# The weighted sum of values in a sliding-window attention tile, done in two halves of places

## The chip, the cores and the metric

The kernel runs on one core of one Trainium2 chip. Its time is the device time of one execution in microseconds (us), given as the median of several executions. TensorE (PE in the profile, its weight loads PEld) multiplies matrices out of SBUF into PSUM; VectorE (DVE) and ScalarE (ACT) work element by element; GpSimd (POOL) and SyncE (SP) do little here but fill tiles and issue transfers (DMAs). PSUM has eight banks per partition; a bank holds 512 float32 numbers per partition.

## The reference, cut to what matters

One decoder layer on x of 2 batches x 512 tokens x 1024: attention, a quantised product with a context, a feed-forward block, each followed by a layer norm. The change lies in the attention alone:

```python
q = (x @ wq.T).reshape(B, N, 32, 128).transpose(0, 2, 1, 3)
k = (x @ wk.T).reshape(B, N, 8, 128).transpose(0, 2, 1, 3)
v = (x @ wv.T).reshape(B, N, 8, 128).transpose(0, 2, 1, 3)
# four query heads share a key/value head; a query i sees the keys j with j <= i and i - j < 128
s = jnp.where((j <= i) & (i - j < 128), (q @ k.T) / sqrt(128), -inf)
o = softmax(s) @ v
x = layernorm(x + o.reshape(B, N, 32 * 128) @ wo.T)
```

## The kernel before, in words

All large products are done by Strassen's scheme (`strassen`, the matmuls on line 132, named `prod`) in float32; the second attention product, with the output weights, is `y` on line 563. In the trace every float32 matmul leaves two records, each with its own weight load ahead of it: a matmul of 512 columns is two records of 512 columns. So 48 matmuls show as x96.

Attention goes over 16 groups (2 batches x 8 key/value heads); a group has four tiles of 128 query tokens (`i` = 0 to 3), and four query heads are handled at once, so a tile of probabilities is 128 x 512. For tile `i`, `scores` (lines 323 to 369) makes the scores in two pairs. Each pair takes the only buffer of the PSUM pool `ps_s`, is copied out by ACT (L348, L350) and, where the diagonal runs through, by DVE under a mask (L352); then maximum, exponential, sum and division follow (L358 to L368).

The window is 128 wide, so query place t of a tile sees t+1 keys of its own tile and 127-t keys of the tile before. The probabilities are therefore kept in a tile with exactly 128 columns: column j holds the key j of the own tile for j <= t, and the key j of the tile before for j > t.

`weigh` (lines 384 to 404) does the weighted sum one tile later. `transpose_p` turns the probabilities with four transposes into the only buffer of the PSUM pool `ps_t` (tile `pt`, L374). DVE writes `cur`, in which only the entries of keys of the own tile are left (L380, a product with the mask `keep_cur`), and ACT writes `both`, all entries (L381). Then two matmuls add up in one bank of `ps_t` (tile `o`): values of the tile before times `both` (L397), and the difference `vd` of own and earlier values times `cur` (L398), which corrects the entries that belong to the own tile. For `i` = 0 there is one matmul (L395). One ACT copy (L401) takes the result, 128 x 512, into the tile `factors`. After every second tile, `keep` forms sums for the later product on DVE (L408 to L413) and stores them through SP's queue (L424). There are 16 x 3 = 48 weighings with two matmuls and 16 with one.

Once per group, `transpose_v` (lines 305 to 312) turns the values of the next group with four transposes into the same single buffer of `ps_t` (tile `vtr`, L308); ACT copies them out whole (L310, 128 x 512), and DVE forms `vd` from the copy (L312, 128 x 384). It falls between the `pt` and the `o` of the weighing with `i` = 0, in all groups but the first set-up: `pt`, `vtr` and `o` take the one buffer in turn.

Around this, `other` (line 446) feeds in steps of the next group's projections and of the output product, so that TensorE has work while ACT and DVE do the softmax. Each engine works through its own queue strictly in the order that the framework laid down when the program was built; that order follows the framework's own estimate of when operands are ready, so it isn't the order of the Python code: in the trace, products stand between the `pt` and the `o` of a weighing.

PSUM is full: two banks `ps_p`, four `ps_y`, one `ps_s`, one `ps_t`.

Of the kernel before, what the change touches and what calls it, by code (L numbers as in the profile page):

```python
# [9 lines left out]
F32 = mybir.dt.float32  # L10
# [4 lines left out]
ALU = mybir.AluOpType  # L15
# [3 lines left out]
P = 128  # L19
# [6 lines left out]
TPB = N // P  # L26
NQ = 32
NKV = 8
G = NQ // NKV
# [11 lines left out]
RND = 8388608.0  # L41
QMID = 128.0
MASKED = -3.0e38
HQ = HALF // 2


# [134 lines left out]
class Background:  # L181
# [6 lines left out]
    def add(self, steps, share=1):  # L188

        self.queue.append([steps, share, 0])  # L190
# [18 lines left out]
def attention(nc, tc, consts, xbuf, tpool, wpool, ps_p, ps_y, dram, kept, complete, between):  # L209
# [7 lines left out]
    with ExitStack() as ctx:  # L217
        qpool = ctx.enter_context(tc.tile_pool(name="a_q", bufs=2))
        kvpool = ctx.enter_context(tc.tile_pool(name="a_kv", bufs=2))
        work = ctx.enter_context(tc.tile_pool(name="a_work", bufs=2))  # L220
        ps_s = ctx.enter_context(tc.tile_pool(name="ps_s", bufs=1, space=PSUM))
        ps_t = ctx.enter_context(tc.tile_pool(name="ps_t", bufs=1, space=PSUM))

        factors = ctx.enter_context(tc.tile_pool(name="a_factors", bufs=1)).tile([P, 7, 7, P], F32, tag="factors", name="factors")
# [36 lines left out]
        x0 = load_x(0)  # L261
        load_weight(1)

        qT, kT, vT, v, vd = {}, {}, {}, {}, {}

        def project_first(outs):

# [37 lines left out]
        def transpose_v(b, g):  # L305
            ps = ps_t.tile([P, TPB, P], F32, tag="t", name=f"vtr_{b}_{g}")
            for i in range(TPB):
                nc.tensor.transpose(ps[:, i, :], vT[b, g][:, ts(i, P)], ident)  # L308
            v[b, g] = kvpool.tile([P, TPB, P], F32, tag="v", name=f"v_{b}_{g}")
            nc.scalar.copy(v[b, g], ps)  # L310
            vd[b, g] = kvpool.tile([P, TPB - 1, P], F32, tag="vd", name=f"vd_{b}_{g}")
            nc.vector.tensor_tensor(vd[b, g], v[b, g][:, 1:], v[b, g][:, : TPB - 1], ALU.subtract)  # L312

        def pieces(m):

            b, g = groups[m]
            for j in range(PAIRS):
                yield from project(m * PAIRS + j)
                if j == 0:
                    transpose_v(b, g)  # L320
                    yield

        def scores(b, g, i, meanwhile):
# [6 lines left out]
            if i == 0:  # L330
                nc.gpsimd.memset(s, MASKED)
            for pair in range(G // 2):
# [38 lines left out]
        def transpose_p(b, g, i, s):  # L371
            ps = ps_t.tile([P, G, P], F32, tag="t", name=f"pt_{b}_{g}_{i}")
            for c in range(G):
                nc.tensor.transpose(ps[:, :, ts(c, BLOCK)], s[:, c, :], ident)  # L374
            cur = work.tile([P, G, P], F32, tag="cur", name=f"cur_{b}_{g}_{i}", bufs=1)
            if i == 0:
                nc.scalar.copy(cur, ps)
                return cur, None
            both = work.tile([P, G, P], F32, tag="both", name=f"both_{b}_{g}_{i}", bufs=1)
            nc.vector.tensor_tensor(cur, ps, keep_cur.unsqueeze(1).to_broadcast([P, G, P]), ALU.mult)  # L380
            nc.scalar.copy(both, ps)  # L381
            return cur, both

        def weigh(pending, meanwhile):


            if pending is None:
                meanwhile()
                return
            b, g, i, s = pending  # L390
            cur, both = transpose_p(b, g, i, s)
            meanwhile()
            ps = ps_t.tile([P, G, P], F32, tag="t", name=f"o_{b}_{g}_{i}")
            if i == 0:
                nc.tensor.matmul(ps, v[b, g][:, 0, :], cur, start=True, stop=True)  # L395
            else:
                nc.tensor.matmul(ps, v[b, g][:, i - 1, :], both, start=True, stop=False)  # L397
                nc.tensor.matmul(ps, vd[b, g][:, i - 1, :], cur, start=False, stop=True)  # L398
            half, place = divmod(i, 2)
            keeping.drain()  # L400
            nc.scalar.copy(factors[:, 2 * half : 2 * half + 2, 2 * place : 2 * place + 2],  # L401
                           ps.rearrange("p (k j) t -> p k j t", k=2))
            if place:
                keeping.add(keep(b, g, half))

# [9 lines left out]
        def keep(b, g, half):  # L415


            own = slice(2 * half, 2 * half + 2)
            yield from left_sums(*(factors[:, own, k] for k in range(7)))
            if half:  # L420
                yield
                yield from left_sums(*(factors[:, k] for k in range(7)), True)
            for k in (3, 4, 5, 2, 6) if half else (0, 1):
                nc.sync.dma_start(out=kept[b][:, g, k], in_=factors[:, k])  # L424
            if half:
                complete.add((b, g, "kept"))
            yield

        keeping = Background()
# [4 lines left out]
        for m, (b, g) in enumerate(groups):  # L434
            if m + 2 == NKV:
                x1 = load_x(1)
            if m + 1 == NKV:

                right[1], late = strassen_right_steps(nc, tpool, x1, "t_1")
                late = list(late)  # L440
                for _ in range(2):
                    late.pop(0)()
            rest = pieces(m + 1) if m + 1 < len(groups) else iter(())
            for i in range(TPB):

                def other():
                    lump = next(rest, None)
                    if late:
                        late.pop(0)()
                        lump = LUMP  # L450
                    between(b, g, i, lump, keeping)

                s = scores(b, g, i, other)
                weigh(pending, other)
                pending = b, g, i, s
                for _ in range(STEPS - 2):
                    other()
            for _ in rest:
                pass
        weigh(pending, lambda: between(B - 1, NKV - 1, TPB, None, keeping))  # L460
        keeping.drain()


def project_out(nc, tc, b, xres, spaces, psum, kept, complete, wo_d, sums, x_d, begun):
# [20 lines left out]
    def load_right(n):  # L485
        if n < len(steps):
            k, g = steps[n]
            rights[n] = stream.tile([P, 2, 2, HQ], F32, tag="right", name=f"or_{b}_{n}")
            src = wo_d[(0, 2, 3)[k - 1]] if k <= 3 else sums[:, k - 4]
            nc.sync.dma_start(out=rights[n].rearrange("p j e c -> p j (e c)"), in_=src[:, g])  # L490

    def right_sums(n):
# [6 lines left out]
        b11, b12, b21, b22 = (right[:, j, e] for j in range(2) for e in range(2))  # L499
        t = stream.tile([P, 3, HQ], F32, tag="sums", name=f"ot_{b}_{n}", bufs=2)  # L500
        t1, t2, t4 = (t[:, j] for j in range(3))
# [17 lines left out]
    yield  # L519
    banks = [psum.tile([P, 2, HQ], F32, tag="p", name=f"y{k}_{b}") for k in range(4)]  # L520

# [3 lines left out]
    def read(k):  # L525
        w = stream.tile([P, 4, HQ], F32, tag="right", name=f"yw_{b}_{k}")
        p1, u4, u2, u3 = (w[:, j] for j in range(4))
        q1, q6, q7, q5 = banks[0][:, 0], banks[0][:, 1], banks[1][:, 0], banks[3][:, 1]
        add = lambda out, in0, in1: nc.vector.tensor_tensor(out, in0, in1, ALU.add)
        nc.scalar.copy(p1, q1)  # L530
        tc.keep_in_program_order(add(u2, q6, p1))
        add(u3, q7, u2)
        add(u4, q5, u2)
        rows = w[:, 0:2], u3.unsqueeze(1).to_broadcast([P, 2, HQ])
        grown = banks[2], banks[3]
        whole = w[:, 0:2], w[:, 2:4]
        for q in range(2):
            add(whole[q], grown[q], rows[q])
        yield LUMP
        for n, (h, e) in enumerate(grow[k][1]):  # L540
            for q in range(2):
                block = x[:, 2 * h + q, ts(e, HALF)].rearrange("p (e c) -> p e c", e=2)
                last = add(block, whole[q], block)
                if q == 0:
                    tc.keep_in_program_order(last)
            if n == 0:
                yield LUMP
# [445 lines left out]
def decoder_layer(ctx, tc, x, xT, ctx_kv, wq, wk, wv, wo, s1, z1, s2, z2, wgu, wgu_rest, wd, out):  # L993
# [150 lines left out]
    def prepare_feed_forward():  # L1144

        for u in range(2):
            if u not in left:
# [3 lines left out]
    ahead.add(sum_output_weights())  # L1151
    ahead.add(sum_weights())
    attention(nc, tc, (ident, mask_i, keep_cur), xbuf, tpool, wpool, pools[3], ps_y,
              (xT, wq, wk, wv), kept, complete, in_attention)
    aside.drain()
# [68 lines left out]
```

## Time and profile before

| | |
|---|---|
| median of three runs | 1901.31 us (1899.17 to 1902.37) |
| the profiled execution | 1899.1 us, span of its program 1897.4 us |
| mean granted TensorE clock | 0.998 |
| TensorE busy | 1870.3 us (99%), 8666 matmul records |
| weight loads busy | 1548.1 us (82%) |
| VectorE busy | 1370.6 us (72%) |
| ScalarE busy | 562.6 us (30%) |
| attention (scores and weighings) | 45 to 1016 us of the span |

A row of a group of instructions gives line, engine, operation, tiles (out<-in), their tile of the array, their shape and count; then busy time and the mean ns of one; then the engine's idle time just before them and what ended it. A matmul's end is modelled and reaches past the start of the next one, so the spacing of starts tells what a matmul costs in a dense stream. A row of the timeline gives start and length in us, engine, line, operation, tiles and count, and in brackets the idle time before it.

### The profile page before, as it was taken

How to read it: one execution, taken by the hardware profiler on the slowest of the kernel's cores; microseconds unless marked ns; L12 is line 12 of the kernel's file. 1: busy time of each engine (PE TensorE's matmuls, PEld its weight loads, DVE VectorE, ACT ScalarE, POOL GpSimd, SP SyncE). 2: the span in 40 equal slices, each digit the busy share in tenths (PEclk: the TensorE clock that was granted, in tenths of full speed). 3: DMA queues.
4: the chain of work that ended last, by engine and by line, in shares of the span. 5: the costliest groups of instructions: out<-in, count | busy, mean ns of one | idle time of the engine just before them, and what ended most of it. 6: DMA issues, size and time to landing. Idle time of an engine off the chain costs nothing.

```text
span 1897.4 us, 24656 instructions
## 1 busy us (share of the span) xinstructions
PE 1870.3 (99%) x8666; PEld 1548.1 (82%) x8678; DVE 1370.6 (72%) x3021; ACT 562.6 (30%) x1571; POOL 13.8 (1%) x32
## 2 busy tenths in 40 slices
PE   9999999999999999999999999999999999999997
PEld 6888888878888888888777888888788778888885
DVE  4678888787777676767787667767777697655657
ACT  1334433332211221233543111112233244321224
POOL 0000000000000000000000000000000000000000
PEclk9999999999999999999999999999999999999999
DMA  8478888777888888856368777766344244544431
GB/s 310 170 263 287 287 280 289 263 242 255 276 305 273 277 284 287 273 187 224 115 213 287 264 274 249 261 239 211 122 152 147 84 158 170 200 139 134 166 128 45
DMA packets 183323, 416.88 MB, mean 220 GB/s; under 512 B 16672, under 2 KB 93728, under 8 KB 183200
## 3 DMA queue, kind: packets, MB, share of 16 engines
q1 hardware_dynamic: 181760, 412.94, 63.5%
q10 hardware_dynamic: 1440, 2.36, 0.3%
q8 instruction: 69, 1.13, 0.2%
q14 instruction: 54, 0.44, 0.1%
HBM read 318.77 MB, written 96.47 MB: 219 GB/s over the span
## 4 chain that ended last, share of the span: by engine, by line
PE 84%; DVE 10%; ACT 3%; DMA 2%; issue 1%; SPq 0%; DVEq 0%; ACTq 0%
PE prod L132 49%; PE y L563 16%; PE d L818 7%; PE ps L338 3%; PE o L397 2%; PE o L398 2%; PE m L686 1%; PE pt L374 1%; DMA wd<-in_wd_dram 1%; PE first L273 1%; PE o L395 1%; ACT s L362 1%; DMA ol<-kept 1%; DVE factors L409 0%; DVE lo L774 0%
## 5 line engine op out<-in xcount | busy, mean ns | idle before, releaser
L563 PE MATMUL y<-or,ol 128*128 128x256 f32 x896 | 243.6, 379 | 1.3 <-DMA ol<-kept 1.2
L563 PEld LDWEIGHTS y<-or,ol 128*128 128x128 f32 x896 | 169.0, 190 | 28.0 <-issue 3.6
L563 PE MATMUL y<-ot,ol 128*128 128x256 f32 x672 | 184.3, 382 | 1.8 <-DVE ot L507 1.5
L132 PE MATMUL prod<-xT,w 128*128 128x256 f32 x752 | 182.7, 380 | 0.1
L132 PE MATMUL prod<-t,w 128*128 128x256 f32 x752 | 177.2, 379 | 0.0
L132 PE MATMUL prod<-t,s 128*128 128x256 f32 x752 | 176.7, 379 | 0.1
L132 PE MATMUL prod<-x2T,wgu 128*128 128x256 f32 x672 | 160.1, 380 | 0.2 <-DMA sgu<-sums 0.2
L132 PEld LDWEIGHTS prod<-t,w 128*128 128x128 f32 x752 | 140.1, 190 | 23.6 <-issue 6.7
L132 PE MATMUL prod<-t,wgu 128*128 128x256 f32 x672 | 159.4, 379 | 0.0
L132 PEld LDWEIGHTS prod<-xT,w 128*128 128x128 f32 x752 | 139.4, 190 | 24.3 <-issue 6.7
L132 PEld LDWEIGHTS prod<-t,s 128*128 128x128 f32 x752 | 140.3, 190 | 23.1 <-issue 4.8
L132 PE MATMUL prod<-t,sgu 128*128 128x256 f32 x672 | 155.7, 379 | 0.5 <-ACT g L154 0.5
L563 PEld LDWEIGHTS y<-ot,ol 128*128 128x128 f32 x672 | 124.8, 190 | 27.3 <-DVE ot L507 6.4
L132 PEld LDWEIGHTS prod<-x2T,wgu 128*128 128x128 f32 x672 | 127.3, 190 | 18.9 <-ACT g L154 0.6
L132 PEld LDWEIGHTS prod<-t,wgu 128*128 128x128 f32 x672 | 127.2, 190 | 18.9 <-issue 0.5
L132 PEld LDWEIGHTS prod<-t,sgu 128*128 128x128 f32 x672 | 127.2, 190 | 18.8 <-ACT g L154 0.9
L362 ACT ACTIVATE s<-s,top 128x128 f32<-128x128 f32 x256 | 99.6, 390 | 34.0 <-DVE top L359 33.2
L818 PE MATMUL d<-hi,act 128*128 128x512 f32 x256 | 108.6, 425 | 0.4 <-DVE act L798 0.2
L348 ACT COPY s<-ps 128x128 f32<-128x128 f32 x192 | 39.5, 232 | 228.1 <-PE ps L338 228.0
L832 DVE TENSOR_TENSOR acc<-d,acc 128x512 f32<-128x512 f32 x104 | 71.1, 690 | 43.5 <-PE d L818 43.1
L818 PE MATMUL d<-lo,act 128*128 128x512 f32 x256 | 101.1, 395 | 0.0
L157 DVE TENSOR_TENSOR st<-prod,st 128x256 f32<-128x256 f32 x89 | 37.5, 422 | 83.0 <-PE prod L132 82.7
(220 smaller groups left out, 2983.5 us busy)
## 6 DMA issues: line engine op xcount, KB each, us to landing
kept<-factors SPq DMA_DIRECT2D x112, 448.0 KB, 3.6
ol<-kept SPq DMA_DIRECT2D x112, 448.0 KB, 5.3
w<-in_wq_dram SPq DMA_DIRECT2D x64, 512.0 KB, 4.6
or<-wo_sums SPq DMA_DIRECT2D x64, 512.0 KB, 5.1
sgu<-sums SPq DMA_DIRECT2D x42, 768.0 KB, 6.4
or<-in_wo_dram SPq DMA_DIRECT2D x48, 512.0 KB, 4.6
wgu<-in_wgu_dram SPq DMA_DIRECT2D x42, 512.0 KB, 4.1
wd<-in_wd_dram SPq DMA_DIRECT2D x42, 512.0 KB, 3.5
```

The lines of the kernel that those rows point to most:

```text
L132: nc.tensor.matmul(ps, left[k - 1][:, c, :], right[k - 1][:, c, :], start=start and c == 0, stop=c == KH - 1, skip_group_check=True)
L157: nc.vector.tensor_tensor(u3, two, p1, ALU.add)
L273: nc.tensor.matmul(ps[h][:, part], weights[0][:, h, c], x0[:, c, part], start=c == 0 and k == 0, stop=c == KC - 1, skip_group_check=True,)
L338: nc.tensor.matmul(ps[:, k, cut // BLOCK : G + 1].rearrange("p d w -> p (d w)"), qT[b, g][:, G * i + c].rearrange("p h w -> p (h w)"), kT[ ...
L348: nc.scalar.copy(s[:, c, c * BLOCK :], ps[:, k, : G - c].rearrange("p d w -> p (d w)"))
L362: nc.scalar.activation(s[:, h, :], s[:, h, :], AF.Exp, bias=top[:, h : h + 1], scale=QSCALE, accum_out=total[:, h : h + 1],)
L374: nc.tensor.transpose(ps[:, :, ts(c, BLOCK)], s[:, c, :], ident)
L397: nc.tensor.matmul(ps, v[b, g][:, i - 1, :], both, start=True, stop=False)
L398: nc.tensor.matmul(ps, vd[b, g][:, i - 1, :], cur, start=False, stop=True)
L563: nc.tensor.matmul(banks[bank][:, half], left[:, SLOT[j]], mine[j], start=grow[k][0] and g == 0 and half == 0, stop=g == LAST, skip_group_ ...
L818: nc.tensor.matmul(ps, act[:, ts(i, P)], half[:, part], start=start and k == 0, stop=stop and k == len(parts) - 1)
L832: nc.vector.tensor_tensor(acc[t][:, ts(e, HALF)], ps, acc[t][:, ts(e, HALF)], ALU.add)
```

## The change

For tiles `i` >= 1 the 512 columns (4 heads x 128 places) are split in two halves of places, 4 x 64 columns each. For the first 64 places, only keys 0 to 63 of the own tile can be seen, so the base product uses the earlier tile's values, as before, and the correction needs only rows 0 to 63. For the last 64 places all keys 0 to 63 are of the own tile and only keys 64 to 127 can be of either; the base product uses a mixed tile (rows 0 to 63 from the own tile, rows 64 to 127 from the earlier one), and the correction needs only rows 64 to 127.

So the two matmuls of 128 rows x 512 columns become four of 256 columns: two of 128 rows and two of 64 rows, these two in different halves of the array's rows. The first half's result stays in `ps_t`; the second half's goes to a tile of `ps_s`, the pool of the scores. The copy into `factors` becomes two ACT copies of 128 x 256. `transpose_v` makes three ACT copies out of PSUM instead of one (the values without the last tile, 128 x 384, and the mixed tiles in two copies of 64 partitions x 384), and DVE forms `vd` with one operand straight from PSUM.

```diff
+RH = P // 2
...
-            v[b, g] = kvpool.tile([P, TPB, P], F32, tag="v", name=f"v_{b}_{g}")
-            nc.scalar.copy(v[b, g], ps)
+            both = kvpool.tile([P, 2, TPB - 1, P], F32, tag="v", name=f"v_{b}_{g}")
+            v[b, g], mixed[b, g] = both[:, 0], both[:, 1]
+            nc.scalar.copy(v[b, g], ps[:, : TPB - 1])
+            nc.scalar.copy(mixed[b, g][:RH], ps[:RH, 1:])
+            nc.scalar.copy(mixed[b, g][RH:], ps[RH:, : TPB - 1])
             vd[b, g] = kvpool.tile([P, TPB - 1, P], F32, tag="vd", name=f"vd_{b}_{g}")
-            nc.vector.tensor_tensor(vd[b, g], v[b, g][:, 1:], v[b, g][:, : TPB - 1], ALU.subtract)
+            nc.vector.tensor_tensor(vd[b, g], ps[:, 1:], v[b, g], ALU.subtract)
...
-            ps = ps_t.tile([P, G, P], F32, tag="t", name=f"o_{b}_{g}_{i}")
+            half, place = divmod(i, 2)
+            out = factors[:, 2 * half : 2 * half + 2, 2 * place : 2 * place + 2]
             if i == 0:
+                ps = ps_t.tile([P, G, P], F32, tag="t", name=f"o_{b}_{g}_{i}")
                 nc.tensor.matmul(ps, v[b, g][:, 0, :], cur, start=True, stop=True)
+                keeping.drain()
+                nc.scalar.copy(out, ps.rearrange("p (k j) t -> p k j t", k=2))
             else:
-                nc.tensor.matmul(ps, v[b, g][:, i - 1, :], both, start=True, stop=False)
-                nc.tensor.matmul(ps, vd[b, g][:, i - 1, :], cur, start=False, stop=True)
-            half, place = divmod(i, 2)
-            keeping.drain()
-            nc.scalar.copy(factors[:, 2 * half : 2 * half + 2, 2 * place : 2 * place + 2],
-                           ps.rearrange("p (k j) t -> p k j t", k=2))
+                ps = [pool.tile([P, G, RH], F32, tag=tag, name=f"o{k}_{b}_{g}_{i}") for k, (pool, tag) in enumerate(((ps_t, "t"), (ps_s, "s")))]
+                for k, values in enumerate((v, mixed)):
+                    nc.tensor.matmul(ps[k], values[b, g][:, i - 1, :], both[:, :, ts(k, RH)], start=True, stop=False)
+                for k in range(2):
+                    own = ts(k, RH)
+                    nc.tensor.matmul(ps[k], vd[b, g][own, i - 1, :], cur[own, :, own], start=False, stop=True)
+                keeping.drain()
+                for k in range(2):
+                    nc.scalar.copy(out[:, :, :, ts(k, RH)], ps[k].rearrange("p (k j) t -> p k j t", k=2))
```

More of the change, by code (lines that the diff above doesn't have):

```diff
@@ L262, in attention @@
         load_weight(1)
-        qT, kT, vT, v, vd = {}, {}, {}, {}, {}
+        qT, kT, vT, v, mixed, vd = {}, {}, {}, {}, {}, {}
         def project_first(outs):
```

## The prediction

> **What bounds the kernel now.** I read the page first (engines, then the chain that ended last), then the groups of instructions with shapes kept apart, then the timeline around single weighings. The page's engine shares and chain:
>
> ```profile
> PE 1870.3 (99%) x8666; PEld 1548.1 (82%) x8678; DVE 1370.6 (72%) x3021; ACT 562.6 (30%) x1571; POOL 13.8 (1%) x32
> ...
> PE 84%; DVE 10%; ACT 3%; DMA 2%; issue 1%; SPq 0%; DVEq 0%; ACTq 0%
> PE prod L132 49%; PE y L563 16%; PE d L818 7%; PE ps L338 3%; PE o L397 2%; PE o L398 2%; PE m L686 1%; PE pt L374 1%; DMA wd<-in_wd_dram 1%; PE first L273 1%; PE o L395 1%; ACT s L362 1%; DMA ol<-kept 1%; DVE factors L409 0%; DVE lo L774 0%
> ```
>
> TensorE's queue is the bound: what the change puts into or takes out of it moves the end one for one; ACT and DVE matter only where TensorE waits for them. The two lines that the change rewrites hold 4% of the chain. The same lines by shape, with a product as a yardstick:
>
> ```profile
> L132 PE MATMUL prod<-t,s 128*128 128x256 f32 x752 | 176.7, 379 | 0.1
> L132 PEld LDWEIGHTS prod<-t,s 128*128 128x128 f32 x752 | 140.3, 190 | 23.1 <-issue 4.8 <-ACT a1T L680 0.3 <-ACT kT L154 0.3
> L397 PE MATMUL o<-both,v 128*128 128x512 f32 x96 | 49.7, 600 | 0.3 <-ACT both L381 0.3
> L398 PE MATMUL o<-cur,vd 128*128 128x512 f32 x96 | 49.0, 592 | 0.0
> ```
>
> The reader is to see 96 records for 48 matmuls (two passes each, each with its own load), and that every load and matmul of this program takes the whole array (128*128): nothing here runs on half of the rows. The timeline around one weighing that had to wait, and its restart:
>
> ```profile
> 763.27 0.59 PE L563 MATMUL y<-or,ol 128*128 128x256 f32 x2
> 763.50 0.59 ACT L381 COPY both<-pt 128x512 f32<-128x512 f32 x1 [3.57 <-DVE top L359]
> 764.14 0.30 PEld L397 LDWEIGHTS o<-both,v 128*128 128x128 f32 x2 [0.68 <-ACT both L381]
> 764.14 1.13 PE L397 MATMUL o<-both,v 128*128 128x512 f32 x2 [0.28 <-ACT both L381]
> 765.10 1.02 PE L398 MATMUL o<-cur,vd 128*128 128x512 f32 x2
> 765.96 0.59 PE L563 MATMUL y<-ot,ol 128*128 128x256 f32 x2
> ```
>
> From 765.10 to 765.96 the pair of passes of L398 takes 0.86 us, 0.43 a pass. From 764.14 to 765.10 the pair of L397 takes 0.96: 0.10 more, because its first weight load was not hidden under an earlier matmul. So an exposed load costs 0.10 us. And the one place where PSUM's single `ps_t` buffer is handed on under pressure:
>
> ```profile
> 355.84 0.60 PE L308 MATMUL vtr<-ident,vT 128*128 128x128 f32 x4
> 356.27 1.03 PE L132 MATMUL prod<-xT,w 128*128 128x256 f32 x4
> 356.47 0.61 ACT L310 COPY v<-vtr 128x512 f32<-128x512 f32 x1
> 357.14 0.30 PEld L395 LDWEIGHTS o<-cur,v 128*128 128x128 f32 x2 [0.24 <-ACT v L310]
> 357.14 1.12 PE L395 MATMUL o<-cur,v 128*128 128x512 f32 x2
> 357.50 0.55 DVE L312 TENSOR_TENSOR vd<-v 128x384 f32<-128x384 f32 x1
> ```
>
> `o` starts 0.06 us after the copy of the values has freed the bank, and four product records (4 x 0.216 = 0.86) were laid between to cover the wait.
>
> **The change part by part.** The sum is against the profiled execution's 1899.1 us (span 1897.4); the median of the three runs is 2.2 us above it, which I add at the end.
>
> *Base products.* Per weighing, two passes of 512 columns (2 x 0.43 = 0.86 us) become four of 256. Product records of that shape start every 0.216 us: from 356.27 the four above give 0.86. So 4 x 0.216 = 0.86: no change. Two loads more, 0.19 each, lie under 0.216 of matmul, as for all products: nothing, while that cover holds.
>
> *Corrections.* Two passes of 512 columns (0.86 us) become four of 256 columns and 64 rows. One after the other they take 0.86 again: halving the rows halves no time by itself. A gain comes only if matmuls in the two halves of the rows run at once. Passes of one half use the same rows and follow each other; queue order is first half pass 1, pass 2, second half pass 1, pass 2, so if starts stay in order only the middle two meet: three slots, a gain of 0.216 per weighing, 48 x 0.216 = 10.4 us. Bounds: no overlap, 0; all passes in pairs, 0.43, or 20.7 us. I take 10.4.
>
> *Going to half rows and back.* Each weighing switches the array from whole to half rows and back, 96 switches. The trace shows no switch. Lower bound: nothing (0), as between the transposes and products above, which follow with no gap. Upper bound: the switch waits until earlier matmuls have run out and then loads with no cover. A product record lasts 0.379 and the next starts after 0.216, so the tail is 0.163; with an exposed load 0.10, 0.26 per switch, 25 us in all. I take the exposed load and half the tail, since that modelled tail also holds reading and writing that may overlap: 0.10 + 0.08 = 0.18 per switch, 96 x 0.18 = 17.3 us. Against the gain: 17.3 - 10.4 = +6.9 us.
>
> The Trainium skill speaks for this price: "TensorEngine Tiling (Array Packing)", Key Properties, says that changing the tiling mode, not only the tile, drains TensorE. Taken at its word, with the full tail, it would make it 25 - 10.4 = +14.6 us. It speaks for the gain too: "TensorE: Matmul & The Clock Gate", Part 3, gives 3.07x for four row tiles of K=32, all in one mode; with that alone, the sum would be about -10 us. No row here shows either.
>
> *Turning the values.* ACT goes from one copy of 128x512 (0.583) to three of 384 columns. A copy of 128x256 takes 0.37 (row of `st`, L143), so 384 lie between 0.37 and 0.58; halfway is 0.48. ACT gets 3 x 0.48 - 0.58 = +0.85 us, 16 times: 14 us on an engine that is 30% busy. `vd` keeps its shape; a DVE operand in PSUM costs no more (`cur` from PSUM 128x512 0.683, L368 from SBUF 0.685). But `vd` now reads the bank, and DVE and ACT take turns on one (ACT's `both` waited for DVE's `cur` 38 times, though both only read `pt`). So the bank comes free not after 0.61 us but after 1.43 + 0.55, about 1.3 us later, in front of L395, 15 times; the four records no longer cover it and everything behind in TensorE's queue would wait. Bounds: 0, if six more product records are laid between, and 15 x 1.3 = 20 us if none. The order is laid for modelled readiness, and the four records show that it fills such waits: I take one restart, 15 x 0.07 = +1 us.
>
> *Copies out and the score bank.* L401 (0.583) becomes two of 0.37: +0.16 us of ACT, 48 times, 7.5 us, hidden under products; DVE's sums behind it (L408) waited for L401 7.6 us in 6 cases, so about 1 us moves on DVE, which TensorE doesn't see. SP's stores behind these sums shift as little. `o`'s second half needs the scores' only bank. At 333 us the masked copy of the last scores (L352) ends at 332.40 and L397 starts at 333.10; the next scores start at 338.27, 2.7 us after the end of L401 at 335.61, and the later copy takes 0.2 to 0.4 of it. In most weighings this is free; five late ones have under 1 us, at most 5 x 0.4 = 2 us, I take 0.
>
> Sum: 1899.1 + 6.9 + 1 = 1907.0; with the 2.2 us, 1909.
>
> **The rivals.** *Halves overlap, switches are free* (ends faster): one mechanism, the middle passes of L398's successor run side by side and the loads for half the rows are fetched ahead as now. -10.4 + 1 us: 1892. It decides as soon as a switch costs under 0.11 us (10.4/96); for it speaks the gapless step from transposes to products; against it that those also use all 128 rows. *Switch costs only the exposed load*: 96 x 0.10 = 9.6 against 10.4: 1901, no difference. *No overlap, and full switches*: +25 + 1: 1927; for it, that nothing here shows overlap. *TensorE waits for `vtr`'s bank*: the planner fills nothing, +20 on top of a free exchange: 1890 + 20, some 1911 to 1915; against it, the four records.
>
> **How the numbers follow.** 0.2%, or 3.8 us, is about what a measurement here can tell from none. Chances: forecast (switch 0.13 to 0.22 each, +3 to +12 us) 0.40; free switches 0.30; load only 0.14; full switch or no overlap 0.10; bank 0.06. The forecast's own range is 1904 to 1913. Eight in ten reach from free switches, 1892 less 2 for their own spread, to beyond the switch's upper bound with the gain, 25 - 10.4 = +14.6 or 1899.1 + 14.6 + 1 + 2.2 = 1917, so 1919; above lies the case without overlap, below a fuller overlap. Slower: 0.37 of the forecast's 0.40, with 0.10 and 0.06: 0.53. Same: 0.14 with 0.03, less 0.03 that falls to the faster side: 0.14. Faster: 0.33.
>
> **What would show it.** Half-row records, 192 of them for the corrections, and the distance from the first base pass to the next program step: 1.72 now, forecast 1.72 - 0.216 + 0.37 = 1.87; 1.51 would mean free switches, 2.2 no overlap with full switches. Starts of the second and third half-row pass within some 10 ns mean overlap. The first half-row load should start after the last base pass has run out, and not under it. L395 after `vtr`: ten product records between instead of four, and an idle time before its load as now. DVE and ACT busier by about 0 and 21 us. The forecast falls if loads for half the rows are still fetched ahead, if all four half-row passes pair up, or if the queue's order shifts elsewhere.

## The result, and the profile after

The changed kernel takes 1906.95 us (median of 8 runs, 1905.37 to 1910.28), the kernel before 1900.89 (8 runs, 1898.32 to 1903.74): a ratio of 1.0036 (95% interval 1.0027 to 1.0045), or 6.1 us more. The forecast was 1909 with 1890 to 1919. The profiled execution of the changed kernel is the slowest of its eight (1910.28, span 1908.5); the trace is read for single places, and the medians for the time.

The page of the changed kernel, engine shares and the chain that ended last:

```profile
PE 1874.7 (98%) x8857; PEld 1559.3 (82%) x8870; DVE 1370.6 (72%) x3021; ACT 579.0 (30%) x1651; POOL 13.8 (1%) x32
...
PE 79%; DVE 13%; ACT 3%; DMA 3%; issue 2%; SPq 0%; DVEq 0%; ACTq 0%
PE prod L133 46%; PE y L577 15%; PE d L832 7%; PE ps L343 3%; PE o L410 2%; PE o L413 2%; DMA wd<-in_wd_dram 1%; PE pt L379 1%; PE m L700 1%; ACT s L367 1%; PE first L274 1%; DVE factors L422 1%; DMA raw<-in_wgu_dram 1%; DMA ol<-kept 1%; PE o L402 1%
```

TensorE is still the bound, but its share of the chain fell from 84% to 79%, and DVE's rose from 10% to 13%: the chain runs more often through something that TensorE waits for. ACT is 16 us busier (21 forecast), DVE not at all. The groups of the changed lines, by shape:

```profile
L410 PE MATMUL o<-both,v 128*128 128x256 f32 x192 | 51.3, 383 | 1.8 <-ACT both L386 1.7
L413 PE MATMUL o<-cur,vd 64*128 64x256 f32 x192 | 37.9, 428 | 0.0
L413 PEld LDWEIGHTS o<-cur,vd 64*128 64x128 f32 x192 | 16.2, 184 | 17.7 <-issue 14.2 <-DVE or L518 1.0 <-DVE xres L543 0.7
```

The 96 half-row corrections leave 192 records, all on half of the rows (64*128). Their records last 428 ns each, longer than a full one of as many columns (383), but the engine is busy with all of them for only 37.9 us, 0.20 a record: they lie on top of each other. Before the loads of each stay in half rows the load queue stands idle for some 0.33 us (17.7 us in 54 stays). Most of that still lies under the last full pass; what it costs TensorE is read from the starts. One weighing in the timeline of the changed kernel (the fourth line is from a narrower window and holds the second passes alone):

```profile
334.90 1.03 PE L410 MATMUL o<-both,v 128*128 128x256 f32 x4
335.86 0.30 PEld L413 LDWEIGHTS o<-cur,vd 64*128 64x128 f32 x4 [0.33 <-issue]
335.86 0.70 PE L413 MATMUL o<-cur,vd 64*128 64x256 f32 x4
336.18 0.38 PE L413 MATMUL o<-cur,vd 64*128 64x256 f32 x2
336.49 0.51 PEld L133 LDWEIGHTS prod<-t,w 128*128 128x128 f32 x3 [0.33 <-issue]
336.49 0.70 PE L133 MATMUL prod<-t,w 128*128 128x256 f32 x2
```

The four base passes start every 0.216 us, and their slots end at 334.90 + 4 x 0.216 = 335.77 (with the unrounded start). The first half-row load starts only at 335.86: 0.09 us in which nothing starts, then 0.11 for a load with no cover. Two first passes start together (7 ns apart), two second passes at 336.18 (again 7 ns), and the loads of the second ones are hidden. The two of a pair must belong to different halves, for where one half runs alone (next fence) its two passes start 0.32 us apart. The product's load after them starts at 336.49, 0.09 after the last slot (336.19 + 0.216 = 336.40), and again 0.11 goes on an uncovered load: in the trace the product's first record is followed by the next after 0.320, and not 0.216. In all 0.86 + 0.20 + 0.43 + 0.20 = 1.69 us, where the two full matmuls took 1.72. So the switch costs 0.2 us each way, the overlap gives 0.43, and a weighing is 0.03 us shorter, not longer.

In 6 of 48 weighings it isn't so: there the order laid the two corrections apart. In five of them the masked copy of the last scores, which frees the scores' bank, ended only 0.6 to 1.8 us after the first half had started, as here (timeline of the changed kernel):

```profile
646.46 0.59 PE L410 MATMUL o<-both,v 128*128 128x256 f32 x2
646.99 0.70 PE L413 MATMUL o<-cur,vd 64*128 64x256 f32 x2
647.61 1.13 PE L133 MATMUL prod<-xT,s 128*128 128x256 f32 x4
647.68 0.22 DVE L357 COPY_PREDICATED s<-mask_i,ps 128x64 f32<-128x64 int32 x1
648.58 0.59 PE L410 MATMUL o<-both,v 128*128 128x256 f32 x2
649.11 0.70 PE L413 MATMUL o<-cur,vd 64*128 64x256 f32 x2
649.73 1.13 PE L133 MATMUL prod<-xT,s 128*128 128x256 f32 x4
```

The masked copy (L357) is the last reader of the scores' bank; only after it does the second half go. In the sixth, at 323 us, the bank had been free for over 4 us; there a product of another part of the layer (`cs`, L668) stands between the two corrections. The array is sent to half rows twice and nothing overlaps: each half takes 647.61 - 646.46 = 1.15, with the load after it 1.25, together 2.51 us, 0.79 more than before. 42 x -0.03 + 6 x 0.79 is +3.4 us; summed over the trace, the weighings take 86.1 us against 82.4.

The exchange of the weighings' bank, after:

```profile
357.16 0.60 PE L309 MATMUL vtr<-ident,vT 128*128 128x128 f32 x4
357.60 1.46 PE L133 MATMUL prod<-xT,w 128*128 128x256 f32 x6
357.80 0.51 ACT L313 COPY v<-vtr 128x384 f32<-128x384 f32 x1
358.18 0.48 ACT L314 COPY v<-vtr 64x384 f32<-64x384 f32 x1
358.67 0.47 ACT L315 COPY v<-vtr 64x384 f32<-64x384 f32 x1
358.90 1.03 PE L133 MATMUL prod<-t,s 128*128 128x256 f32 x4
359.18 0.56 DVE L317 TENSOR_TENSOR vd<-vtr,v 128x384 f32<-128x384 f32 x1
359.79 0.30 PEld L402 LDWEIGHTS o<-cur,v 128*128 128x128 f32 x2 [0.27 <-DVE vd L317]
```

Three copies and the difference come one after the other; in 6 of the 16 groups DVE stood idle until the third copy was through (2.7 us in all). `o` starts 2.2 us after the transposes' slots end, 1.3 later than before, and ten product records lie between, not four. In each of the 15 groups with this exchange at least six more lie there than before.

The rest of the loss is a handful of longer waits elsewhere. From the first start of the scores to the last start of a weighing, the attention takes 970.6 us in the trace before (45.0 to 1015.6) and 980.9 in the trace after (44.6 to 1025.5), 10.4 more by the unrounded starts. 3.7 us of it are the weighings, so some 6.7 us are later starts elsewhere. The four longest that are new stand at 979 us (1.6), 470 (1.5), 643 (1.3) and 931 (1.0). At 470 and 643 DVE waits for a transfer and TensorE for DVE. At the other two TensorE waits for ACT (timeline of the changed kernel):

```profile
977.36 0.60 PE L379 MATMUL pt<-ident,s 128*128 128x128 f32 x4
978.77 0.60 ACT L386 COPY both<-pt 128x512 f32<-128x512 f32 x1
979.42 0.70 PE L410 MATMUL o<-both,v 128*128 128x256 f32 x2 [1.47 <-ACT both L386]
...
930.67 0.62 ACT L416 COPY factors<-o 128x256 f32<-128x256 f32 x2
931.34 0.30 PEld L343 LDWEIGHTS ps<-kT,qT 128*128 128x128 f32 x2 [1.24 <-ACT factors L416]
```

At 979 nothing was laid between the transposes and the weighing. At 931 the next scores wait until ACT has copied the second half out of their bank.

### The profile page after: what moved, and what is told of

Same layout as the page of the kernel before. It is cut to its first block, busy times and chain, and to the rows that moved or that the text cites. A ratio compares the mean times of both kernels' runs of the same rounds, so it can differ in the third digit from the quotient of the medians.

```text
span 1908.5 us, 25124 instructions
## 1 busy us (share of the span) xinstructions
PE 1874.7 (98%) x8857; PEld 1559.3 (82%) x8870; DVE 1370.6 (72%) x3021; ACT 579.0 (30%) x1651; POOL 13.8 (1%) x32
## 3 DMA queue, kind: packets, MB, share of 16 engines
q8 instruction: 70, 1.15, 0.2%
## 4 chain that ended last, share of the span: by engine, by line
PE 79%; DVE 13%; ACT 3%; DMA 3%; issue 2%; SPq 0%; DVEq 0%; ACTq 0%
PE prod L133 46%; PE y L577 15%; PE d L832 7%; PE ps L343 3%; PE o L410 2%; PE o L413 2%; DMA wd<-in_wd_dram 1%; PE pt L379 1%; PE m L700 1%; ACT s L367 1%; PE first L274 1%; DVE factors L422 1%; DMA raw<-in_wgu_dram 1%; DMA ol<-kept 1%; PE o L402 1%
## 5 line engine op out<-in xcount | busy, mean ns | idle before, releaser
L800 ACT ACTIVATE sg<-g 128x512 f32<-128x512 f32 x43 | 27.2, 632 | 231.7 <-DVE g L175 231.6
```

The lines of the kernel that those rows point to most:

```text
L800: nc.scalar.activation(a, g, AF.Sigmoid, scale=1.0 / 128.0)
```

## The experiments

Each run's ratio is to the kernel before on the same chip, with its 95% interval. The first four runs shared a chip, so did the next three, and so did the three after them; across these groups the ratios compare better than the medians.

| run | median us | ratio |
|---|---|---|
| changed kernel again | 1905.70 | 1.0029 (1.0017 to 1.0041) |
| pairs pinned | 1904.62 | 1.0025 (1.0015 to 1.0034) |
| full rows | 1904.63 | 1.0019 (1.0010 to 1.0028) |
| halves apart | 1939.18 | 1.0206 (1.0192 to 1.0220) |
| one bank, full rows | 1903.27 | 1.0019 (1.0010 to 1.0028) |
| bank freed | 1907.64 | 1.0045 (1.0031 to 1.0059) |
| pinned and freed | 1904.93 | 1.0028 (1.0018 to 1.0039) |
| values' turning alone | 1901.85 | 1.0012 (1.0003 to 1.0021) |
| split of columns alone | 1902.17 | 1.0009 (1.0000 to 1.0018) |
| two copies out alone | 1900.81 | 1.0002 (0.9993 to 1.0011) |
| pair twice | 1924.62 | 1.0135 (1.0119 to 1.0152) |

**The changed kernel again.**

> The changed kernel once more, to see which of its waits come back. Its first trace gave, per weighing with both corrections side by side, 1.693 us of TensorE time against 1.72 before (-0.03), and 2.51 us (+0.79) for the 6 of 48 weighings whose two halves the order laid apart: 42 x -0.03 + 6 x 0.79 = +3.4 us, and single waits beside it. Theory A (split weighings and waits for the shared PSUM banks make the loss): some 6 us over the kernel before, the 6 splits and the waits at the scores again in the same places. Theory B (the forecast: going to half rows and back costs more than the overlap gives, in every weighing): the same time, but then each weighing would have to take 1.87 us. A wait for a transfer at 470 us (1.5 us) is not expected again by either.

The 6 splits came back, and so did the waits at the scores (642 us, 1.3; 930 us, 1.0) and at the weighing at 978 us (1.6). The wait at 470 us came back too (1.3 us), against the expectation: it belongs to this order of the queues, not to chance. The attention takes 979.3 us this time, 980.9 in the first trace, so 1.6 us of such a length is run to run.

**Halves apart.** The price of a split weighing, by making all of them split (`keep_in_program_order` pins an instruction behind the one written just before it):

```diff
-                for k, values in enumerate((v, mixed)):
-                    nc.tensor.matmul(ps[k], values[b, g][:, i - 1, :], both[:, :, ts(k, RH)], start=True, stop=False)
-                for k in range(2):
-                    own = ts(k, RH)
-                    nc.tensor.matmul(ps[k], vd[b, g][own, i - 1, :], cur[own, :, own], start=False, stop=True)
+                for k, values in enumerate((v, mixed)):
+                    own = ts(k, RH)
+                    first = nc.tensor.matmul(ps[k], values[b, g][:, i - 1, :], both[:, :, own], start=True, stop=False)
+                    if k:
+                        tc.keep_in_program_order(first)
+                    tc.keep_in_program_order(nc.tensor.matmul(ps[k], vd[b, g][own, i - 1, :], cur[own, :, own], start=False, stop=True))
```

> The changed kernel with every weighing laid as base and correction of the first half, then base and correction of the second, so that no two corrections run side by side and TensorE goes to half rows twice per weighing. Theory A: 42 weighings go from 1.69 to 2.51 us, +34 us, about 1941. Theory B (three slots instead of four by the middle passes, 0.18 us a switch): +0.22 for the lost overlap and +0.37 for two more switches, 42 x 0.59 = +25 us, 1932. If overlap and switches were both worth little: under +10 us.

1939.2: 33.5 us over the changed kernel's 1905.7, as the two prices say (34), and not the 25 of three slots with cheaper switches. The half-row records of this run, in the groups by shape:

```profile
L414 PE MATMUL o<-cur,vd 64*128 64x256 f32 x192 | 67.3, 431 | 0.0
L414 PEld LDWEIGHTS o<-cur,vd 64*128 64x128 f32 x192 | 28.5, 186 | 32.0 <-issue 24.3 <-DVE top L364 4.6 <-DVE ot L517 0.7
```

The same 192 records keep TensorE busy for 67.3 us instead of 37.9, and their loads leave 32.0 us idle before them instead of 17.7.

**Pair twice.** The opposite: a second pair where the array is in half rows already.

```diff
-                for k in range(2):
-                    own = ts(k, RH)
-                    tc.keep_in_program_order(nc.tensor.matmul(ps[k], vd[b, g][own, i - 1, :], cur[own, :, own], start=False, stop=True))
+                for last in (False, True):
+                    for k in range(2):
+                        own = ts(k, RH)
+                        tc.keep_in_program_order(nc.tensor.matmul(ps[k], vd[b, g][own, i - 1, :], cur[own, :, own], start=False, stop=last))
```

> The kernel with pinned pairs (1904.6 us), but each weighing adds its pair of half-row corrections twice in a row, so that the correction is counted double; nothing else is changed. It prices a pair for which the array is in half rows already. Theory A (the second passes' loads are hidden, only going there and back is exposed): two slots of 0.213 us, 48 x 0.43 = +20.5 us, 1925. Rival: every half-row pass keeps the spacing of 0.320 us that the trace shows between first and second pass, 48 x 0.64 = +31 us, 1935. With no overlap it would be 48 x 0.86 = +41 us, 1946.

1924.6, 20.0 us over the pinned pairs' median, 21 by the ratios: two slots of 0.216 for each added pair, so only the way there and back is exposed. In 45 of the 48 weighings all eight records stand together, as here (timeline of this run):

```profile
342.41 1.03 PE L410 MATMUL o<-both,v 128*128 128x256 f32 x4
343.37 0.73 PEld L414 LDWEIGHTS o<-cur,vd 64*128 64x128 f32 x8 [0.33 <-issue]
343.37 1.14 PE L414 MATMUL o<-cur,vd 64*128 64x256 f32 x8
344.43 1.59 PEld L133 LDWEIGHTS prod<-t,w 128*128 128x128 f32 x8 [0.33 <-issue]
```

Eight half-row records from 343.37 to 344.43 take 1.06 us; four took 0.63. The second pair costs 0.43, half of what the same work takes on the whole array.

**Pairs pinned.** The kernel that the run above started from: the changed kernel with pins on its corrections, each added once.

```diff
-                    nc.tensor.matmul(ps[k], vd[b, g][own, i - 1, :], cur[own, :, own], start=False, stop=True)
+                    tc.keep_in_program_order(nc.tensor.matmul(ps[k], vd[b, g][own, i - 1, :], cur[own, :, own], start=False, stop=True))
```

> Each correction is pinned behind the matmul written just before it, so that the two corrections of a weighing stand side by side in TensorE's queue in 47 of 48 weighings instead of 42. Theory A: 5 x 0.79 = 4.0 us off the changed kernel, about 1903. Theory B: nothing, since every weighing still goes to half rows and back: 1907. Rival C (the pair now waits for the bank of the scores instead): between, or slower than 1907.

47 of 48 weighings now have their corrections side by side, and the stretches with half rows take 40.6 us in all instead of 44.6 in the repeat: the 4 us are off the weighings. The one that is still split is the one with `cs` between its corrections; all five with a late bank are mended. The median fell by 1.1 us only (1905.7 to 1904.6, the intervals of the ratios overlap), and the attention in the trace by 2.5 (979.3 to 976.8). That is rival C's side: part of what the pins saved came back as other waits. How large a part stays open; on top of the freed bank (below) the same pins took 2.7 us off the median.

**Full rows.** No half-row instruction left:

```diff
-                for k, values in enumerate((v, mixed)):
+                for k, values in enumerate((v, v)):
...
-                    nc.tensor.matmul(ps[k], vd[b, g][own, i - 1, :], cur[own, :, own], start=False, stop=True)
+                    nc.tensor.matmul(ps[k], vd[b, g][:, i - 1, :], cur[:, :, own], start=False, stop=True)
```

> All as in the changed kernel (two halves of places, the second in the pool of the scores, two copies out, three copies of the values, the mixed tile written but not read), but both base products use the earlier tile's values and both corrections all 128 rows: no half-row instruction is left. Theory A: 42 weighings lose 0.03 and the 6 split ones win 0.79 each: -3.4 us, about 1903.5; what is left over the kernel before (some 3 us) is then waits and order. Theory B: the whole 7 us comes back, 1900.

1904.6, ratio 1.0019. Theory B falls: without a single switch 3.6 us (1.9 to 5.3) of the loss remain. The half rows stand for the difference to the changed kernel, 0.10%, about 2 us; the intervals of the two ratios overlap, and the trace gives them 3.2 us (86.1 - 82.4 = 3.7 by the weighings, less 0.5 for splitting the columns). With the pairs pinned, half rows are no dearer than full ones: the medians are alike (1904.62 and 1904.63), and so is the attention in the traces (976.8 us).

**One bank.** Full rows, and the scores' bank left alone:

```diff
-                ps = [pool.tile([P, G, RH], F32, tag=tag, name=f"o{k}_{b}_{g}_{i}") for k, (pool, tag) in enumerate(((ps_t, "t"), (ps_s, "s")))]
-                for k, values in enumerate((v, mixed)):
-                    nc.tensor.matmul(ps[k], values[b, g][:, i - 1, :], both[:, :, ts(k, RH)], start=True, stop=False)
-                for k in range(2):
-                    own = ts(k, RH)
-                    nc.tensor.matmul(ps[k], vd[b, g][own, i - 1, :], cur[own, :, own], start=False, stop=True)
-                keeping.drain()
-                for k in range(2):
-                    nc.scalar.copy(out[:, :, :, ts(k, RH)], ps[k].rearrange("p (k j) t -> p k j t", k=2))
+                ps = ps_t.tile([P, G, P], F32, tag="t", name=f"o_{b}_{g}_{i}")
+                for k in range(2):
+                    nc.tensor.matmul(ps[:, :, ts(k, RH)], v[b, g][:, i - 1, :], both[:, :, ts(k, RH)], start=k == 0, stop=False, skip_group_check=True)
+                for k in range(2):
+                    nc.tensor.matmul(ps[:, :, ts(k, RH)], vd[b, g][:, i - 1, :], cur[:, :, ts(k, RH)], start=False, stop=True, skip_group_check=True)
+                keeping.drain()
+                nc.scalar.copy(out, ps.rearrange("p (k j) t -> p k j t", k=2))
```

> As the run with full rows, but both halves of places write their columns of one tile in the weighings' own PSUM bank and leave by one copy of 128x512, as before the change; the scores' bank is left alone. The values are still turned as in the changed kernel (three copies out of PSUM, the difference from PSUM; the mixed tile is written, not read). Theory D (taking the scores' only bank for the second half makes the late order): the +0.19% of the full-rows run goes, 1900 to 1901, and the waits of the scores at 641 and 928 us and of the weighing at 977 us are gone. Theory E (the values' longer hold on the weighings' bank makes it): stays at about 1904.

The same 1.0019. The changed kernel's waits at 930 and 978 us are gone, but the one of the scores at 640 us is there without any use of their bank (1.8 us). Theory D falls as the cause of the rest: with full rows, the scores' bank costs nothing that these runs can tell (each ratio is known to 0.09%, 1.7 us). With half rows it does, through five of the 6 splits.

**Bank freed, and both edits.** The values leave PSUM in one copy:

```diff
-            nc.scalar.copy(v[b, g], ps[:, : TPB - 1])
-            nc.scalar.copy(mixed[b, g][:RH], ps[:RH, 1:])
-            nc.scalar.copy(mixed[b, g][RH:], ps[RH:, : TPB - 1])
+            nc.scalar.copy(v[b, g], ps)
+            nc.scalar.copy(mixed[b, g][:RH], v[b, g][:RH, 1:])
+            nc.scalar.copy(mixed[b, g][RH:], v[b, g][RH:, : TPB - 1])
...
-            nc.vector.tensor_tensor(vd[b, g], ps[:, 1:], v[b, g], ALU.subtract)
+            nc.vector.tensor_tensor(vd[b, g], v[b, g][:, 1:], v[b, g][:, : TPB - 1], ALU.subtract)
```

> The changed kernel, but the values leave PSUM by one copy of 128x512 as before, and the mixed tile and the difference are made from the copy in SBUF, so that the bank is free after one copy. Theory E: about 1 to 3 us off the changed kernel, 1903 to 1905, and the waits of the turned values at 206 and 255 us (0.4 us each) gone. Theory D: no difference, 1906.

> The changed kernel with both edits: corrections of a weighing pinned side by side, and the values' bank freed after one copy. Theory D: as with pinned pairs alone, 1904 to 1905. Theory E: 1901 to 1902. Neither expects it below the kernel before by more than the 48 x 0.03 = 1.4 us that pairs save.

The bank is handed on as before the change, after one copy and four records (timeline of the run with the bank freed):

```profile
357.87 0.60 PE L309 MATMUL vtr<-ident,vT 128*128 128x128 f32 x4
358.31 1.03 PE L133 MATMUL prod<-xT,w 128*128 128x256 f32 x4
358.51 0.61 ACT L313 COPY v<-vtr 128x512 f32<-128x512 f32 x1
359.17 0.30 PEld L402 LDWEIGHTS o<-cur,v 128*128 128x128 f32 x2 [0.24 <-ACT v L313]
```

But nothing is won: 1.0045 against 1.0029, and with pinned pairs 1.0028 against 1.0025. The waits before the turned values at 206 and 255 us are still there (0.40 and 0.36 us). Theory E's 1 to 3 us don't show; the edit lays the queues anew as well (the product with the output weights at 471 us now waits 2.1 us, not 1.5), so a small gain at the bank could be hidden under that. Neither run beats the kernel before, and no other did.

**The parts alone.** Three single edits of the kernel before. The values' turning is the change's own lines of `transpose_v`; the other two are:

```diff
-                nc.tensor.matmul(ps, v[b, g][:, i - 1, :], both, start=True, stop=False)
-                nc.tensor.matmul(ps, vd[b, g][:, i - 1, :], cur, start=False, stop=True)
+                for k in range(2):
+                    own = ts(k, P // 2)
+                    nc.tensor.matmul(ps[:, :, own], v[b, g][:, i - 1, :], both[:, :, own], start=k == 0, stop=False, skip_group_check=True)
+                for k in range(2):
+                    own = ts(k, P // 2)
+                    nc.tensor.matmul(ps[:, :, own], vd[b, g][:, i - 1, :], cur[:, :, own], start=False, stop=True, skip_group_check=True)
```

```diff
-            nc.scalar.copy(factors[:, 2 * half : 2 * half + 2, 2 * place : 2 * place + 2],
-                           ps.rearrange("p (k j) t -> p k j t", k=2))
+            for own in (slice(None),) if i == 0 else (ts(0, P // 2), ts(1, P // 2)):
+                nc.scalar.copy(factors[:, 2 * half : 2 * half + 2, 2 * place : 2 * place + 2, own],
+                               ps[:, :, own].rearrange("p (k j) t -> p k j t", k=2))
```

> The kernel before, with only the turning of the values taken from the change (three ACT copies out of PSUM, the mixed tile written and not read, the difference from PSUM). Theory E (the longer hold on the bank costs): the +0.19% that full rows and one bank both still had, about 1903. Theory F (that rest comes from any new laying of the queues, by a few longer waits in the products and the scores that fall where a transfer is late): between 0 and +4 us, not to be told from the next two runs.

> The kernel before, with only the matmuls of a weighing split into four of 256 columns and all 128 rows, in the one bank, one copy out. By the trace four records of 256 columns take what two of 512 take (1.728 against 1.718 us), 48 x 0.01 = 0.5 us. Theory E: 1900. Theory F: 0 to +4 us.

> The kernel before, with only the copy out of a weighing made in two of 128x256. ACT gets 7 us more, on an engine 30% busy, and TensorE does not see it. Theory E: 1900. Theory F: the queues are laid anew, 0 to +4 us. If all three runs of this call stay at 1900, neither explains the rest and it is left open.

+0.12%, +0.09% (its interval starts at zero) and +0.02%; the first two add up to about the 0.19% that full rows and one bank had. None costs TensorE that much in its own instructions (nothing, 0.5 us and nothing). In one trace of each the attention is longer by 1.8, 4.5 and 0.3 us. Part of the difference sits in a few places where the new order meets a late transfer. In the run with the split of columns, the queue reaches a product with the output weights while its operand `ot` is late, for DVE waits behind a transfer (timeline of that run):

```profile
465.78 0.43 DVE L506 TENSOR_TENSOR ot<-or 128x256 f32<-128x256 f32 x1 [1.73 <-DMA sums<-sum]
467.13 0.42 DVE L507 TENSOR_TENSOR ot<-or,ot 128x256 f32<-128x256 f32 x1
467.61 0.70 PE L567 MATMUL y<-ot,ol 128*128 128x256 f32 x2 [1.86 <-DVE ot L507]
```

In the run with the values' turning alone, it is the scores that wait for DVE, and DVE for a transfer:

```profile
638.01 0.42 DVE L1110 TENSOR_TENSOR sum<-raw 128x256 f32<-128x256 f32 x1 [1.50 <-DMA raw<-in_wgu_dram]
639.48 0.22 DVE L356 COPY_PREDICATED s<-mask_i,ps 128x64 f32<-128x64 int32 x1
639.76 0.68 PE L342 MATMUL ps<-kT,qT 128*128 128x160 f32 x3 [1.27 <-DVE s L356]
```

Neither wait is in the kernel before; both are in the changed one (1.5 us at 470, 1.3 at 643). The run with two copies out was laid anew as well and has neither (it has one of 1.5 us at 994 instead, behind a transfer, and no loss that its ratio shows): a new order doesn't always lose. Why these edits lead to such an order, and whether another laying of the same instructions would be free of it, stays open: theory F is supported, not shown. As far as these runs tell, the 6.1 us are some 1 to 3 us by half rows, through the 6 split weighings (1.1 and 2.7 by the pins, 2 by full rows, 3.2 by the trace), and 3.6 us (1.9 to 5.3) by the edits around them, through waits.

## Why the prediction was right, and where it was not

The side and the size were right (+6.1 measured, +8 forecast against the median), the range held, but the path was another. That the sum came near is luck: the half rows, forecast at +6.9, came to +3.4 in the trace, all of it by split weighings that the forecast put at nothing, and waits that it left out filled the gap.

- *Base products*: four passes at 0.216 for two at 0.43: right (41.5 us for all against 41.2), and loads stay hidden among them.
- *Corrections*, the mis-sized term: the forecast took "three slots, a gain of 0.216", because the queue's order seemed to let only the middle passes meet. The trace shows two slots: the first passes of both halves start 7 ns apart, then both second passes. The gain is 0.43, the upper bound given. Whether the queue holds the passes in that order or the engine takes them so, the records don't say. "TensorE: Matmul & The Clock Gate" of the Trainium skill, Part 3, has matmuls of distinct row groups start some 4 ns apart; here it is 7, and within one mode (the pair twice) the factor is two. The -10 us that the prediction sets beside that page is its own three slots without switches, and isn't worked out from the page's 3.07x.
- *Going to half rows and back*: 0.18 taken, 0.20 measured (0.09 with nothing started and 0.11 of uncovered load each way). Right, and the forecast's split (exposed load 0.10 and half the tail 0.08) is near each part. "TensorEngine Tiling (Array Packing)" of the Trainium skill, Key Properties, says that a change of mode drains the engine; the trace agrees in that nothing starts for 0.09 us a time.
- So a weighing with its pair takes 1.69 us, not the forecast 1.87, and with all 48 so this term would have been -1.4 us instead of +6.9. What made it a loss was unforeseen: 6 split weighings at +0.79. The step that failed is "five late ones have under 1 us, at most 5 x 0.4 = 2 us, I take 0": the late bank costs the pairing, and with it a second way there and back, in five weighings (the sixth split has another cause). It costs a wait as well: at 931 us the next scores stand 1.0 us behind ACT's copy out of their bank.
- *Turning the values*: bank 1.3 us later, ten records in place of four, no longer wait at L395's successor (4.3 us in all before, 3.7 after): right in each. The 1 us taken came out as 2.3 (0.6 to 4.0) by the values' turning alone, with no sign that it is lost at that bank: freeing it early won nothing.
- *Copies out*: hidden, right where they leave the weighings' own bank (0.02%, -0.07 to 0.11). Out of the scores' bank they aren't always, as the wait at 931 us shows.
- Left out altogether: that every edit lays all queues anew, and that a new order can meet late transfers, or leave TensorE with nothing between two steps, at places that have little to do with the change. By the run with full rows this took 3.6 of the 6.1 us.
- The rivals: switches were not free (0.11 us was the point of decision, 0.20 measured); two of them at 0.20 just break even with the fuller overlap of 0.43. "No overlap" is what the split weighings show.

## What to carry to other kernels

In this kernel two matmuls on the two halves of the rows ran at once and halved their time, but each stay in half rows costs about 0.4 us on a dense TensorE stream: it pays only where the work within one stay saves clearly more than that, so collect pairs before going there, and pin them side by side. A pair that needs two PSUM banks at the same moment is only as safe as the later bank. In a kernel whose queues are laid by estimates, an edit that costs nothing by itself can move the whole through the new order (here by 0 to 0.2%), so measure a gain of that size against such edits.

## What the runs showed of the hardware that was not expected

- Of two float32 half-row matmuls in a row, each of two passes, the first passes run together and then the second passes (starts 7 ns apart, then 0.320 us later again 7 ns apart); a second pair of matmuls right behind costs 0.43 us, its passes starting every 0.216 us.
- A half-row record of 256 columns is listed with 428 ns, a full one with 383, though a new one starts every 0.216 us in a row: the listed length of a record is no measure of its slot.
- Leaving half rows costs as much as entering: 0.09 us with nothing started, and then a load of 0.11 us that isn't covered.
